# Loading the second block's input first, and one square root for two norms, in a Mamba + MLP + mixture-of-experts kernel

## The chip, the cores and the metric

The kernel runs on one core of a Trainium2 chip. A core has a matrix engine (TensorE, PE in the profile, with its weight loads as PEld), a vector engine (VectorE, DVE), an engine for functions such as exp, silu and square root (ScalarE, ACT), a general engine (GpSimd, POOL) and a queue engine that here only issues transfers (SyncE, SP). Each takes its instructions in the order in which they stand in its queue; semaphores tie the engines together. The metric is the device time of one execution in microseconds (us).

## The reference

Input x is 2048 tokens by 512, all in float32. Cut to what matters:

```
x = x + ref1(layernorm(x))        # Mamba-2 block, then a gated MLP
x = x + ref2(layernorm(x))        # router, 8 experts, the best 2 of each token

ref1(h):
  r = h;  h = rmsnorm(h, ln1_w)
  z, xb, B, C, dt = split(h @ in_proj_w)
  xb, B, C = silu(causal_conv4([xb, B, C]))
  dt = softplus(dt + dt_bias);  A = -exp(A_log)
  y = scan over chunks of 128 tokens of (xb*dt, dt*A, B, C) + D*xb
  h = r + rmsnorm(y * silu(z), norm_w) @ out_proj_w
  return h + (silu(h2 @ gate_w) * (h2 @ up_w)) @ down_w,  h2 = rmsnorm(h, ln2_w)

layernorm(x)  = (x - mean) / sqrt(var + eps)
rmsnorm(h, w) = h / sqrt(mean(h*h) + eps) * w          # eps = 1e-5 in both
```

Two norms follow each other at the start: layernorm of x, then rmsnorm of its result. With v the variance of a token, layernorm scales by `rstd = 1/sqrt(v + eps)`. The mean square of its result is `v * rstd^2`, so both together scale by `rstd / sqrt(v * rstd^2 + eps)`. This is the same as `1 / sqrt(v * (1 + eps) + eps^2)`. The residual path needs `rstd` alone.

## The kernel before

The tokens are cut into 8 blocks of 256 (`TB`), each of two tiles of 128. The Mamba part runs block by block. For every group of 512 tokens (`FB`) the gated MLP and the router are interleaved, with one group's lag: while blocks 0 and 1 (the first group) run, there is no MLP work yet. After the last block come the rest of the MLP and the experts. The script names dependencies only; a planner puts the instructions of each engine in a fixed order ahead of the run, by its own model of times and by the order of the script. An instruction that the script has late can stand early in its queue when its inputs are ready early in that model.

The start, by lines:

- L79 to L100 issue the first loads on the queue of SP: two x tiles (`load_x`, L77, 256 KB each), the parameters (L86), the columns of w_in for dt (`w_dt`, L88), three column pairs of w_in (`load_w_in`, L93, 512 KB each, four buffers), two more x tiles for block 1, then `w_o` (L99, 2 MB) and the router's weights (L100).
- L135 and L136 compute `a_neg = -exp(A_log)`.
- `scales(b)` (L175) takes mean and variance of the block's two tiles into `mv` (`stats`, L148 and L149: DVE), then `rstd` (`rsqrt_eps`, L143: a square root on ACT, L144: a reciprocal on DVE), then `ms = v * rstd^2` (L181, L182), a second `rsqrt_eps` on it, and the product `rboth` (L184).
- `prepare(b)` (L196) is a generator: it calls `scales`, forms `hn = (x - mean) * rboth` (L203), transposes it on PE (L190) and multiplies by ln1_w into `hT` (L194). After a first yield come the projection for dt (`pdt`, L214) and softplus by a polynomial on DVE (L224 to L236), in which the Exp of L226 is the only work of ACT. After a second yield comes `dA = dt * a_neg` (L242), its sum along the chunk on PE (`pc`, L245), and rows that go to memory and come back broadcast (`rowsd`, L250; `cum`, L279, masked on POOL in L281; `ec`, L291).
- `project` (L304) multiplies `hT` by one column pair of w_in (`pm`, L300), copies it to `pre` (L310, ACT), takes three halo columns from the pair's previous block and saves three for the next (L311, L312: POOL), convolves (L317, L319: DVE) and applies silu (L323: ACT). `gate` (L325) does the same product for z (`pz`).
- L457 scales `w_o` by norm_w on POOL, eight instructions, once.
- `chunk` (L338) runs the scan of one tile: `psc` (L361), the exponentials `cum` (L367: ACT, L369: DVE), `py` (L382, L388), `y` (L400, L404), squares on ACT (L424, L425), their sum over eight column groups on POOL (`sq`, L427) and over channels on PE (`pms`, L430), then the output projection `po` (L437). `h` of L439 is layernorm(x), with `rstd`; L440 adds the projection to it.

The loads of later blocks are issued in `mamba(b)`, two blocks ahead (L655). Block 0 is prepared before the loop over blocks (L642), and block b + 1 inside block b.

Of the kernel before, what the change touches and what calls it, by code (L numbers as in the profile page):

```python
# [8 lines left out]
F32 = mybir.dt.float32  # L9
I32 = mybir.dt.int32  # L10
AF = mybir.ActivationFunctionType
ALU = mybir.AluOpType
# [3 lines left out]
P = 128  # L16
# [5 lines left out]
NH = 16  # L22
HD = 64
TB = 256
NCH = TB // P
# [15 lines left out]
EPS = 1e-5  # L41


C_CW, C_CB, C_NW, C_D, C_L1, C_L2, C_DTB, C_AL = 0, 48, 60, 68, 76, 80, 84, 100
# [4 lines left out]
def mamba_mlp_moe(ctx, tc, x, w_in, w_out, w_gate, w_up, w_down, par, wr, wg, wu, wd, out):  # L49
# [3 lines left out]
    nc = tc.nc  # L53

    def bc(ap, axis, n):
        ap = ap.unsqueeze(axis)
        shape = list(ap.shape)
        shape[axis] = n
        return ap.to_broadcast(shape)


    const = ctx.enter_context(tc.tile_pool(name="const", bufs=1))
# [12 lines left out]
    def load_x(t):  # L75
        res[t] = xp.tile([P, D], F32, name=f"x{t}", tag="x")
        nc.sync.dma_start(out=res[t], in_=x[t * P : (t + 1) * P, :])  # L77

    params = const.tile([P, NPAR], F32, name="params")  # L79
# [1 line left out]
    w_o = pw.tile([P, 8, D], F32, name="w_o")  # L81
    wr_sb = const.tile([P, NK, NE], F32, name="wr_sb")

    for t in range(NCH):
        load_x(t)
    nc.sync.dma_start(out=params, in_=par)  # L86
    w_in_k = w_in.rearrange("(k p) n -> p k n", p=P)
# [2 lines left out]
    def load_w_in(pair):  # L90

        w = pw.tile([P, NK, 2 * P], F32, name="wi", tag="wi", bufs=4)
        nc.sync.dma_start(out=w, in_=w_in_k[:, :, pair * 2 * P : (pair + 1) * 2 * P])  # L93
        return w

    ahead = [load_w_in(pair) for pair in range(3)]
    for t in range(NCH, 2 * NCH):
        load_x(t)
    nc.sync.dma_start(out=w_o, in_=w_out.rearrange("(t p) n -> p t n", p=P))  # L99
    nc.sync.dma_start(out=wr_sb, in_=wr.rearrange("(k p) e -> p k e", p=P))  # L100

# [29 lines left out]
        out=upto, in_=ones[:, : NE * NE].rearrange("p (e f) -> p e f", e=NE), pattern=[[1, NE], [-1, NE]],  # L131
        compare_op=ALU.is_ge, fill=0.0, base=0, channel_multiplier=0,
    )
    a_neg = const.tile([P, NH], F32, name="a_neg")
    nc.scalar.activation(a_neg, params[:, C_AL : C_AL + NH], AF.Exp)  # L135
    nc.vector.tensor_scalar_mul(a_neg, a_neg, -1.0)  # L136
    mv = const.tile([P, NT, 2], F32, name="mv")
    rstd = const.tile([P, NT], F32, name="rstd")
    rboth = const.tile([P, NT], F32, name="rboth")

    def rsqrt_eps(dst, src, scale=1.0):

        nc.scalar.activation(dst, src, AF.Sqrt, bias=eps, scale=scale)  # L143
        nc.vector.reciprocal(dst, dst)  # L144

    def stats(pool, src, dst):
        st = pool.tile([P, 6], F32, name="bn", tag="bn")
        nc.vector.bn_stats(out=st, in_=src)  # L148
        nc.vector.bn_aggr(out=dst, in_=st)  # L149
# [7 lines left out]
    wa = pa_stack.enter_context(tc.tile_pool(name="wa", bufs=2))  # L157
# [14 lines left out]
        return pool.tile([P, *shape], F32, name=name, tag=tag)  # L172


    def scales(b):  # L175
        lo, hi = b * NCH, (b + 1) * NCH
        for t in range(lo, hi):
            stats(wa, res[t], mv[:, t, :])
        rsqrt_eps(rstd[:, lo:hi], mv[:, lo:hi, 1])
        ms = wa.tile([P, NCH], F32, name=f"ms{lo}", tag="ms")  # L180
        nc.vector.tensor_tensor(ms, mv[:, lo:hi, 1], rstd[:, lo:hi], ALU.mult)  # L181
        nc.vector.tensor_tensor(ms, ms, rstd[:, lo:hi], ALU.mult)  # L182
        rsqrt_eps(rboth[:, lo:hi], ms)
        nc.vector.tensor_tensor(rboth[:, lo:hi], rboth[:, lo:hi], rstd[:, lo:hi], ALU.mult)  # L184

    def transposed(src, dst, weight=None):

        pt = bank("tr", [NK, P], "pt")
        for k in range(NK):
            nc.tensor.transpose(pt[:, k, :], src[:, k * P : (k + 1) * P], ident)  # L190
        if weight is None:
            nc.scalar.copy(dst, pt)  # L192
        else:
            nc.vector.tensor_tensor(dst, pt, bc(weight, 2, P), ALU.mult)  # L194

    def prepare(b):  # L196

        scales(b)
        hT = wa.tile([P, NK, TB], F32, name=f"hT{b}", tag="hT")
        for j in range(NCH):  # L200
            t = b * NCH + j
            hn = wa.tile([P, D], F32, name=f"hn{t}", tag="tok", bufs=3)
            nc.vector.tensor_scalar(  # L203
                hn, res[t], mv[:, t, 0:1], rboth[:, t : t + 1], ALU.subtract, ALU.mult
            )
            transposed(hn, hT[:, :, j * P : (j + 1) * P], params[:, C_L1 : C_L1 + NK])

        yield hT


        pdt = ps_tr.tile([P, NCH, NH], F32, name=f"pdt{b}", tag="tr")
        for j in range(NCH):
            for k in range(NK):
                nc.tensor.matmul(  # L214
                    pdt[:, j, :], hT[:, k, j * P : (j + 1) * P], w_dt[:, k, :],
                    start=(k == 0), stop=(k == NK - 1),
                )

        def small(name, bufs=2):
            return wa.tile([P, NCH, NH], F32, name=f"{name}{b}", tag=name, bufs=bufs)  # L220

        v, u, s, s2, acc = (small(n, 1) for n in ("v", "u", "s", "s2", "acc"))
        dt = small("dt")
        nc.vector.tensor_tensor(v, pdt, bc(params[:, C_DTB : C_DTB + NH], 1, NCH), ALU.add)  # L224
        nc.vector.scalar_tensor_tensor(u, v, -1.0, v, ALU.mult, ALU.min)
        nc.scalar.activation(u, u, AF.Exp)  # L226
        nc.vector.tensor_scalar_add(s, u, 2.0)
        nc.vector.reciprocal(s, s)
        nc.vector.tensor_tensor(s, s, u, ALU.mult)
        nc.vector.tensor_tensor(s2, s, s, ALU.mult)  # L230
        nc.vector.tensor_scalar_mul(acc, s2, 1.0 / 17.0)
        for c in (15.0, 13.0, 11.0, 9.0, 7.0, 5.0, 3.0):
            nc.vector.scalar_tensor_tensor(acc, acc, 1.0 / c, s2, ALU.add, ALU.mult)
        nc.vector.scalar_tensor_tensor(acc, acc, 1.0, s, ALU.add, ALU.mult)
        nc.vector.tensor_scalar_max(dt, v, 0.0)
        nc.vector.scalar_tensor_tensor(dt, acc, 2.0, dt, ALU.mult, ALU.add)  # L236

        yield


        dA = small("dA")
        nc.vector.tensor_tensor(dA, dt, bc(a_neg, 1, NCH), ALU.mult)  # L242
        n = NCH * NH
        pc = ps_tr.tile([P, P], F32, name=f"pc{b}", tag="tr")
        nc.tensor.matmul(pc[:n], dA.rearrange("p j h -> p (j h)"), tri, start=True, stop=True)  # L245
        rows = wa.tile([n, 2, P], F32, name=f"rows{b}", tag="rows", bufs=1)
        nc.vector.tensor_copy(rows[:, 0, :], pc[:n])
        nc.scalar.activation(rows[:, 1, :], pc[:n], AF.Exp)
        rows_d = scratch.tile([2, n, P], F32, name=f"rowsd{b}", tag="rowsd", bufs=NB)
        nc.sync.dma_start(out=rows_d.rearrange("a n q -> n a q"), in_=rows)  # L250

        pn = ps_tr.tile([P, NCH, NH], F32, name=f"pn{b}", tag="tr")
        nc.tensor.transpose(pn.rearrange("p j h -> p (j h)"), rows[:, 0, :], ident[:n, :n])
        ncum = small("ncum")
        nc.vector.tensor_scalar_mul(ncum, pn, -1.0)

        yield

        dtdec = small("dtdec")
        psum = ps_tr.tile([P, 2, NCH, NH], F32, name=f"psum{b}", tag="tr")  # L260
        nc.tensor.matmul(psum[:, 0], late, dA, start=True, stop=True)
        nc.tensor.matmul(psum[:, 1], ones, dA, start=True, stop=True)
        nc.scalar.activation(dtdec, psum[:, 0], AF.Exp)
        nc.vector.tensor_tensor(dtdec, dtdec, dt, ALU.mult)
        cd = wa.tile([P, NCH, 2, 4], F32, name=f"cd{b}", tag="cd")
        for half in range(2):
            part = slice(half * HD, (half + 1) * HD)
            tot = psum[part, 1].rearrange("p j (g h i) -> p j g h i", g=2, h=2)
            nc.scalar.activation(cd[part], tot[:, :, :, half, :], AF.Exp)
        return hT, dt, ncum, dtdec, cd, rows_d  # L270
# [364 lines left out]
    def finish(steps):  # L635
        while True:
            try:
                next(steps)
            except StopIteration as end:
                return end.value  # L640

    ready = finish(prepare(0))  # L642
    near = [spread(0, j, ready[-1]) for j in range(NCH)]

# [297 lines left out]
```

## Time and profile before

| | us |
|---|---|
| median of 3 runs | 1644.21 (1644.12 to 1644.91) |
| profiled execution, its own time | 1643.64 |
| its span, first to last instruction | 1641.9 |
| PE busy | 1589.6 |
| DVE busy | 706.2 |
| ACT busy | 597.1 |
| POOL busy | 299.4 |
| first matmul or transpose on PE | 13.29 |

The span is what the profile shows; the execution's time is 1.7 us longer. Busy time is summed over the whole span, and the stages differ: at the start and in blocks 0 to 3 several engines are close to full, later PE alone is. Rows of the timeline give start and duration in us, the engine, the line, the operation, what it writes and reads, and how many instructions are merged; in brackets stands how long the engine was idle before it, and what ended that wait. SPq and the like are an engine's queue issuing a transfer. PEclk is the clock of PE that was granted, as a share of full speed.

### The profile page before, as it was taken

The numbers are of one execution on the slowest core, as the hardware profiler recorded it, in microseconds if no ns is written. First come the engines' busy times: TensorE is split into PE (matmuls) and PEld (weight loads), VectorE is DVE, ScalarE is ACT, GpSimd is POOL, SyncE is SP. The second block draws the span as 40 slices with busy tenths as digits, with TensorE's granted clock in tenths as the row PEclk, the third lists the DMA queues.
The fourth block names the chain that finished last, engine by engine and source line by source line (L and its number), as shares of the span: only waits on it lengthen the run. The fifth ranks groups of instructions, "written<-read, shape, count | busy, mean of one in ns | idle before, by whom it ended". The sixth has DMA issues, their size and how long they took to land.

```text
span 1641.9 us, 16534 instructions
## 1 busy us (share of the span) xinstructions
PE 1589.6 (97%) x5515; PEld 909.0 (55%) x5515; DVE 706.2 (43%) x1835; ACT 597.1 (36%) x1033; POOL 299.4 (18%) x349
## 2 busy tenths in 40 slices
PE   6989899999999999999999999999999999999997
PEld 5656565555556655655565555445444655555553
DVE  6776654534445365535544642323421441111111
ACT  4978774435243533353344334112000211111110
POOL 4332211211021102111201110000010123232221
PEclk9999899999999999999999999999999999999999
DMA  7644333434234533333344321228763234333322
GB/s 250 190 115 130 112 116 113 122 91 122 78 115 129 174 97 90 103 110 109 90 146 150 110 71 58 64 64 265 225 206 116 71 58 73 63 59 63 64 40 32
DMA packets 165203, 182.87 MB, mean 111 GB/s; under 512 B 10432, under 2 KB 125632, under 8 KB 165120
## 3 DMA queue, kind: packets, MB, share of 16 engines
q1 hardware_dynamic: 147456, 145.10, 29.9%
q0 software_dynamic: 8736, 20.45, 7.3%
q10 hardware_dynamic: 8928, 16.26, 2.7%
q8 instruction: 46, 0.75, 0.2%
q14 instruction: 37, 0.30, 0.1%
HBM read 155.04 MB, written 26.74 MB: 111 GB/s over the span
## 4 chain that ended last, share of the span: by engine, by line
PE 85%; DMA 4%; issue 4%; ACT 2%; DVE 2%; POOL 1%; SPq 0%; POOLq 0%; DVEq 0%; ACTq 0%
PE pg L592 13%; PE pd L603 13%; PE pu L592 13%; PE pm L300 9%; PE po L437 6%; PE pz L300 5%; PE epd L832 5%; PE epg L817 4%; PE epu L817 4%; DMA out<-ey,idx 3%; PE py L388 2%; PE psc L361 2%; PE py L382 2%; PE pt L190 2%; PE pls L579 1%
## 5 line engine op out<-in xcount | busy, mean ns | idle before, releaser
L592 PE MATMUL pg<-h2T,mg 128*128 128x512 f32 x512 | 231.8, 593 | 0.0
L592 PE MATMUL pu<-h2T,mu 128*128 128x512 f32 x512 | 230.2, 592 | 0.0
L603 PE MATMUL pd<-md,a 128*128 128x512 f32 x512 | 225.4, 592 | 0.0
L300 PE MATMUL pm<-hT,wi 128*128 128x256 f32 x768 | 183.4, 391 | 0.0
L595 DVE TENSOR_TENSOR a<-a,pu 128x512 f32<-128x512 f32 x64 | 44.0, 688 | 285.3 <-PE pu L592 275.8
L603 PEld LDWEIGHTS pd<-md,a 128*128 128x128 f32 x512 | 97.1, 190 | 122.3 <-issue 120.1
L592 PEld LDWEIGHTS pu<-h2T,mu 128*128 128x128 f32 x512 | 97.2, 190 | 122.0 <-issue 117.9
L300 PEld LDWEIGHTS pm<-hT,wi 128*128 128x128 f32 x768 | 145.8, 195 | 34.0 <-issue 12.6
L592 PEld LDWEIGHTS pg<-h2T,mg 128*128 128x128 f32 x512 | 96.1, 190 | 98.6 <-issue 96.3
L606 DVE TENSOR_TENSOR r<-r,pd 128x512 f32<-128x512 f32 x128 | 87.9, 687 | 116.1 <-PE pd L603 115.2
L319 DVE SCALAR_TENSOR_TENSOR ca<-pre,params,ca 128x256 f32<-128x256 f32 x288 | 129.3, 507 | 0.6
L832 PE MATMUL epd<-ew,ehT 128*128 (+1 forms) x234 | 110.2, 607 | 8.5 <-DVE ehT L828 8.5
L437 PE MATMUL po<-w_o,y 128*128 128x512 f32 x256 | 118.4, 610 | 0.0
L817 PE MATMUL epg<-ew,xgT 128*128 x312 | 118.1, 460 | 0.3 <-ACT xgT L192 0.3
L817 PE MATMUL epu<-ew,xgT 128*128 x312 | 117.7, 459 | 0.0
L300 PE MATMUL pz<-hT,wi 128*128 128x256 f32 x512 | 115.1, 381 | 0.0
L300 PEld LDWEIGHTS pz<-hT,wi 128*128 128x128 f32 x512 | 95.5, 190 | 13.6 <-issue 0.8
L819 ACT ACTIVATE eh<-epg 128x352 f32<-128x352 f32 x39 | 18.1, 465 | 218.7 <-PE epg L817 218.7
L367 ACT ACTIVATE cum<-cum,ncum 128x128 f32<-128x128 f32 x256 | 85.1, 391 | 24.1 <-POOL cum L281 23.5
L594 ACT ACTIVATE a<-pg 128x512 f32<-128x512 f32 x64 | 37.7, 588 | 151.8 <-PE pg L592 134.9
L838 POOL DMA_INDIRECT out<-ey,idx x39 | 61.8, 1584 | 160.3 <-DVE ey L837 146.4
L367 ACT ACT_TABLE_LOAD x65 | 83.4, 1283 | 1.6 <-issue 0.6
(220 smaller groups left out, 1777.1 us busy)
## 6 DMA issues: line engine op xcount, KB each, us to landing
wi<-in_w_in SPq DMA_DIRECT2D x80, 512.0 KB, 3.8
mg<-in_w_gate SPq DMA_DIRECT2D x64, 256.0 KB, 2.9
mu<-in_w_up SPq DMA_DIRECT2D x64, 256.0 KB, 2.9
md<-in_w_down SPq DMA_DIRECT2D x64, 256.0 KB, 2.8
cum<-rowsd SPq DMA_DIRECT2D x32, 512.0 KB, 4.8
ec<-rowsd SPq DMA_DIRECT2D x60, 128.0 KB, 4.1
xnd<-xn ACTq DMA_DIRECT2D x28, 256.0 KB, 3.9
ew<-in_wg SPq DMA_DIRECT2D x8, 704.0 KB, 5.5
```

The source lines that it names most:

```text
L300: nc.tensor.matmul(pm[:, m, :], w[:, k, m * P : (m + 1) * P], hT[:, k, :], start=(k == 0), stop=(k == NK - 1))
L319: nc.vector.scalar_tensor_tensor(ca, pre[:, m, k : k + TB], cw[:, k : k + 1], ca, ALU.mult, ALU.add)
L367: nc.scalar.activation(lt[:, half, i], lt[:, half, i], AF.Exp, bias=ncum[:, j, h : h + 1])
L437: nc.tensor.matmul(po, y[:, m, :], w_o[:, m, :], start=(m == 0), stop=(m == 7))
L592: nc.tensor.matmul(ps, wt[:, k, :], hT[:, k, :], start=(k == 0), stop=(k == NK - 1))
L594: nc.scalar.activation(a, pg, AF.Silu)
L595: nc.vector.tensor_tensor(a, a, pu, ALU.mult)
L603: nc.tensor.matmul(pd, a[:, j * P : (j + 1) * P], d, start=(m == 0), stop=(m == len(held) - 1))
L606: nc.vector.tensor_tensor(rows[j], rows[j], pd, ALU.add)
L817: nc.tensor.matmul(ps, xT[:, k, :], w[:, lo : lo + EI], start=(k == 0), stop=(k == NK - 1))
L832: nc.tensor.matmul(pd, hT[:n, m, :], w[:n, NG + m * D : NG + (m + 1) * D], start=(m == 0), stop=(m == len(ET) - 1))
L838: nc.gpsimd.indirect_dma_start(out=out, out_offset=bass.IndirectOffsetOnAxis(ap=idx[:, n : n + 1], axis=0), in_=y, in_offset=None, compute ...
```

## The change

The x tiles of block 1 are loaded together with those of block 0, ahead of the parameters and of w_in. `scales` computes `rboth` directly, with one square root of `v * (1 + eps) + eps^2` and one reciprocal; the constant eps^2 is a new small tile set on POOL. `rstd` is computed by its own square root and reciprocal after the first yield of `prepare`, for every block. `a_neg` is computed in the preparation of block 0, after the second yield, in place of the beginning.

```
-    for t in range(NCH):
+    for t in range(2 * NCH):
         load_x(t)
     nc.sync.dma_start(out=params, in_=par)
...
     ahead = [load_w_in(pair) for pair in range(3)]
-    for t in range(NCH, 2 * NCH):
-        load_x(t)
     nc.sync.dma_start(out=w_o, in_=w_out.rearrange("(t p) n -> p t n", p=P))
...
+    eps2 = const.tile([P, 1], F32, name="eps2")
+    nc.gpsimd.memset(eps2, EPS * EPS)
     a_neg = const.tile([P, NH], F32, name="a_neg")
-    nc.scalar.activation(a_neg, params[:, C_AL : C_AL + NH], AF.Exp)
-    nc.vector.tensor_scalar_mul(a_neg, a_neg, -1.0)
...
     def scales(b):
         lo, hi = b * NCH, (b + 1) * NCH
         for t in range(lo, hi):
             stats(wa, res[t], mv[:, t, :])
-        rsqrt_eps(rstd[:, lo:hi], mv[:, lo:hi, 1])
-        ms = wa.tile([P, NCH], F32, name=f"ms{lo}", tag="ms")
-        nc.vector.tensor_tensor(ms, mv[:, lo:hi, 1], rstd[:, lo:hi], ALU.mult)
-        nc.vector.tensor_tensor(ms, ms, rstd[:, lo:hi], ALU.mult)
-        rsqrt_eps(rboth[:, lo:hi], ms)
-        nc.vector.tensor_tensor(rboth[:, lo:hi], rboth[:, lo:hi], rstd[:, lo:hi], ALU.mult)
+        nc.scalar.activation(rboth[:, lo:hi], mv[:, lo:hi, 1], AF.Sqrt, bias=eps2, scale=1.0 + EPS)
+        nc.vector.reciprocal(rboth[:, lo:hi], rboth[:, lo:hi])
...
         yield hT
+        lo, hi = b * NCH, (b + 1) * NCH
+        rsqrt_eps(rstd[:, lo:hi], mv[:, lo:hi, 1])
...
         yield
+        if b == 0:
+            nc.scalar.activation(a_neg, params[:, C_AL : C_AL + NH], AF.Exp)
+            nc.vector.tensor_scalar_mul(a_neg, a_neg, -1.0)
```

## The prediction

> **What bounds the kernel now.** I read the page first, then busy time by stretch, then the chain of work that ended last, then the start engine by engine, and the waits of TensorE last. The page, engine rows and TensorE by slice:
>
> ```profile
> PE 1589.6 (97%) x5515; PEld 909.0 (55%) x5515; DVE 706.2 (43%) x1835; ACT 597.1 (36%) x1033; POOL 299.4 (18%) x349
> ...
> PE   6989899999999999999999999999999999999997
> ```
>
> TensorE (PE) works 1589.6 of 1641.9 us, so at most 52.3 us can be won. Where its idle time lies, by stretches (busy us of PE, PEld, DVE, ACT, POOL; then clock and DMA):
>
> ```profile
> 0.00:13.29 13.29, 0.00 (x1) 0.04 (x1) 4.73 (x21) 3.37 (x5) 4.68 (x20) 1.00 0.84 270
> 13.29:60.80 47.51, 45.81 (x215) 37.78 (x215) 38.55 (x102) 32.41 (x48) 23.47 (x26) 1.00 0.79 237
> ...
> 112.10:121.00 8.90, 4.30 (x10) 2.86 (x10) 3.37 (x5) 4.42 (x7) 5.32 (x7) 0.67 0.00 0
> ...
> 203.00:1280.00 1077.00, 1075.49 (x3556) 586.07 (x3554) 477.21 (x1235) 384.29 (x645) 135.44 (x176) 1.00 0.40 120
> ```
>
> From 203 to 1280 us PE misses 1.5 us: whatever VectorE (DVE) or ScalarE (ACT) save there is worth nothing. The idle time that the change can reach is the first 13.29 us and the waits before 203. The chain that ended last starts so:
>
> ```profile
> 4.36 6.75 DMA x<-in_x
> 11.13 0.69 DVE bn L148
> ...
> 15.28 3.59 PE pdt L214 x16
> 18.87 5.67 PE pm L300 x16
> ```
>
> The first thing that PE waits for is thus the second block's input, loaded behind three w_in tiles, although block 0 does not need it. DVE, which takes its queue in order, shows why:
>
> ```profile
> 11.13 0.69 DVE L148 BATCH_NORM_STATS2 bn<-x 128x6 f32<-128x512 f32 x1 [3.61 <-DMA x<-in_x]
> 11.74 0.15 DVE L144 RECIPROCAL rboth<-rboth 128x2 f32<-128x2 f32 x1
> ...
> 12.61 0.53 DVE L203 TENSOR_SCALAR hn<-x,mv,rboth 128x512 f32<-128x512 f32 x1
> ```
>
> Block 0's scale (L144) has its root from ACT at 7.85, but stands behind block 1's statistics, which wait for the load.
>
> **The x loads moved.** The queue of SP now issues x0, x1, parameters, w_dt, three w_in, x2, x3; later it is x0 to x3 and then the rest. An issue takes 0.42 to 0.56 us. From 5 to 20 us the DMA runs at 345 to 377 GB/s; take 360, so a 256 KB tile is 0.73 us. x0 was used at 3.56 and x1 at 4.38, so x2 should land near 5.1 and x3 near 5.8, in place of 11.11. Everything they overtake comes up to 1.45 us later: parameters 4.84 to 6.3 (next needed by hT, near 9), w_dt 5.6 to 7.0 (needed near 10). The third w_in: 2.7 MB in front of or in it, 7.5 us at 360, from 2.3 us on: near 10, needed after 13. All are covered; without that cover it is 1.45 us once. w_o, 2 MB, has the same bytes in front of it as before, so its landing, 18.85, does not move.
>
> **One root, and Exp later.** Block 0's chain loses one root (0.29), one reciprocal and three small multiplies (0.13 to 0.17 each). Dropping the A_log Exp from the front also takes a table switch out of the path:
>
> ```profile
> 4.84 0.21 ACT L135 ACTIVATE a_neg<-params 128x16 f32<-128x16 f32 x1 [2.77 <-DMA params<-in_par]
> 5.35 1.28 ACT L143 ACT_TABLE_LOAD   x1 [0.29 <-DVE mv L149]
> 6.64 0.29 ACT L143 ACTIVATE rstd<-mv,eps 128x2 f32<-128x2 f32 x1
> ```
>
> Without Exp the root's table can load at 0.79, and the root follows mv (done at 5.26): ready at 5.6. DVE then does block 1's statistics first if they stay ahead in its queue: x2 until 6.0, x3 until 6.7, an aggregate, reciprocal at 6.9, hn at 7.1. If they do not, hn starts at 5.85. Against 12.61 that is 5.5 or 6.8 us; I take **5.5**, since one of them is ahead now. From hn to pdt the trace needs 15.28 - 12.61 = 2.7 us, so pdt starts near 9.8 and pm near 13.4.
>
> Moving Exp (0.21) and its -1 multiply (0.18) behind dt costs nothing: they are needed by dA (29.29, later 23.8), and ACT is idle for most of the stretch 20 to 28. If Exp needs a table of its own there, 1.28 us, that idle time holds it. The memset of eps2 on POOL is like that of eps, 0.09 us, in front of an idle queue.
>
> rstd still takes a root and a reciprocal, now behind the yield, for h (L440, 82.44 for the first): slack everywhere. Per block there are as many roots, but they no longer depend on each other and can share a table. For block 2 they are now apart, at 37.71 and 42.01, each with a load before and one after; if adjacent, ACT saves 2 x 1.28 = 2.6 us. The Trainium skill (ScalarE: Activation LUTs, What ACT_TABLE_LOAD costs) prices a switch at 1.283 us plus a drain, 2.66 together, which would make it 5.3. The row decides: after the load that starts at 40.72, the root starts at 42.01, with no drain between. I use 1.28.
>
> **What takes the gain back.** The 5.5 us pass on through pdt, dt and dA up to the second column pair of w_in. Its convolution on DVE (L317) waits for the halo copy on POOL, and that stands behind the scaling of w_o:
>
> ```profile
> 18.85 13.42 POOL L457 TENSOR_SCALAR w_o<-w_o,params 128x512 f32<-128x512 f32 x8 [13.52 <-DMA w_o<-in_w_out]
> 32.23 0.19 POOL L312 COPY halo<-pre 128x6 f32<-128x6 f32 x1
> 32.35 0.19 POOL L311 COPY pre<-halo 128x6 f32<-128x6 f32 x1
> ```
>
> ```profile
> 32.58 0.36 DVE L317 TENSOR_SCALAR ca<-pre,params 128x256 f32<-128x256 f32 x1 [0.16 <-POOL pre L311]
> ```
>
> Today this wait is 0.16 us, because statistics of block 2 fill the time. It starts with w_o's landing, which doesn't move; so DVE would arrive near 27 and wait until 32.5. Behind L317 on DVE queue all later convolutions, for which ACT's silu and then PE's psc and py wait. After 32.58 DVE is nearly full until 57.7. What it can still win there is its idle time of 0.82 and 0.69 us (both waiting for ACT, which now is ahead) and four instructions of 0.16: **2.2 us**. If instead the pair's halo copies get in front of w_o, the third pair stops instead: w_o from 20.1 to 33.5, its halo copy at 33.8 against a convolution at 36.73 now: 2.9, plus 0.69 and 0.64, **4.2 us**. The order on POOL can't be read from this trace, so I take the middle, rounded down: **3.0 us**. PE gives back the other 2.5 in waits before psc (49.55) and py (62.29).
>
> Here a rule speaks against the change. The skill (TensorE: Matmul & The Clock Gate, Part 1: The HAM clock gate) says that an idle window of about 3.4 us halves PE's clock until it has been busy as long. The trace agrees at 112 us:
>
> ```profile
> 116.75 0.58 PE L430 MATMUL pms<-ones,sq 128*128 128x1 f32 x2 [4.60 <-POOL sq L427]
> 117.19 2.05 PE L437 MATMUL po<-w_o,y 128*128 128x512 f32 x2
> 119.04 5.08 PE L300 MATMUL pm<-hT,wi 128*128 128x256 f32 x16
> ```
>
> Sixteen pm take 4.89 us in the chain here and 3.54 elsewhere, and two po 1.9 in place of 0.9: 2.4 us of penalty; the wait of 1.5 us before 62.29 brings none. The new waiting is about 2.5 in two pieces, with 1.5 there already, so by the row it costs nothing. By the rule, in one piece it would cost 2.4, leaving 0.6. This is the low end.
>
> **Sum.** Against the profiled execution, 1641.9 of span and 1.7 around it, 1643.64 in all: minus 3.0 is 1640.6. The median of the runs is 0.57 above that execution, so **1641.2** against 1644.2. A difference of 0.2%, 3.3 us, is about what a measurement of this kernel can tell from no change. Its own range is 1639.8 to 1643.6.
>
> **Rivals.**
> *Full carry.* w_o's scaling does not hold the convolution (another order on POOL or DVE), and PE keeps 5.5: 1638.7. For it: PE itself is busy 45.8 of 47.5 us up to 60.8. Against: the 0.16 us wait, already there.
> *The later stalls shrink.* pms at 116.75 and at 197.5 waits for sq on POOL, behind cum (L281), which waits for its DMA. Should the new order put sq first for one, that is 4.6 + 2.4 = 7 more: 1634. The trace has such a case, sq at 152.39 ahead of cum at 161.48. Nothing in the edit aims at it.
> *Slower.* The same place in reverse: at 152 cum gets in front of sq. Then sq ends near 161.48 + 1.09 + 2.6 = 165.2 in place of 155.0; PE has other work for part of that, and I price it like the stall at 112, 7 us: 1641.2 + 7 = 1648. It decides once the new stall takes more than 3.0.
>
> **How the numbers follow.** Partly absorbed 0.55, full carry 0.17, stalls shrink 0.13, slower 0.15. Of the first, 0.4 lies over 3.3 us. Faster: 0.22 + 0.17 + 0.13 = 0.52; same: 0.33 and 0.03 of the slower case, 0.36; slower 0.12. The range, 1635.5 to 1645.5, leaves out about half of the shrunken stalls and two thirds of the slower case.
>
> **What would show it.** Right: the first hn near 7, first pm near 13.4; on DVE's first L317 of the second pair an idle of several us put down to POOL; PE's work at 62.29 only 2 to 4 us earlier; block 2's roots with one load between them; 203 to 1280 as full as now. Wrong: x3 landing after 7; the halo copies ahead of w_o on POOL; the stalls at 112 and 190 gone, longer, or joined by a third.

## The result, and the profile after

| | before | after |
|---|---|---|
| median of 6 runs, us | 1644.86 (1644.12 to 1645.2) | 1635.59 (1633.95 to 1639.16) |
| profiled execution, us | 1643.64 | 1635.68 |
| its span, us | 1641.9 | 1634.0 |
| PE busy, us | 1589.6 | 1587.6 |
| first transpose on PE, us | 13.29 | 10.14 |

The ratio is 0.9948, with a 95% interval of 0.9937 to 0.9960. The kernel is faster by 0.5%, some 8.6 us of the median before.

The page of the kernel after, its engine rows and TensorE by slice:

```profile
PE 1587.6 (97%) x5515; PEld 907.4 (56%) x5515; DVE 700.3 (43%) x1811; ACT 587.6 (36%) x1027; POOL 298.6 (18%) x350
...
PE   7989899999999999999999999999999999999997
```

The idle time of PE, span less busy, fell from 52.3 to 46.4 us; the other 2.0 us of the span are busy time that shrank, since PE worked less at half clock, as shown at the end of this section. Busy time by stretches after, in the columns of the prediction's view:

```profile
0.00:10.14 10.14, 0.00 (x1) 0.03 (x1) 4.71 (x18) 4.11 (x8) 4.71 (x21) 1.00 0.83 263
10.14:60.80 50.66, 48.91 (x225) 38.86 (x226) 37.58 (x106) 34.47 (x56) 22.55 (x26) 1.00 0.80 250
112.09:121.00 8.91, 8.91 (x34) 6.13 (x35) 3.00 (x8) 4.25 (x8) 1.82 (x3) 0.81 0.20 57
...
203.00:1280.00 1077.00, 1074.13 (x3532) 582.60 (x3531) 475.55 (x1221) 377.15 (x637) 134.84 (x174) 1.00 0.40 119
```

The empty stretch at the start is 3.15 us shorter. From 203 to 1280 us PE misses 2.9 us where it missed 1.5. Followed along PE's work, the change is ahead of the kernel before by: 3.2 us at the first transpose, 5.1 at the first `py` (62.29 to 57.17), 5.8 at the first `pms` (77.62 to 71.84), 4.7 at the second and at the third, 7.0 at the fourth (197.52 to 190.53), 8.9 at the first `pg`, the first product of the gated MLP (217.91 to 209.04), and 7.9 at the end. Not all of these marks have the same work in front: ahead of the first `py` the kernel before has done 48 `pz` and the change 44, ahead of the first `pms` 6 and 4 `po`, ahead of the third and the fourth two `po` fewer than the change. The `psc` behind the first `py` has the same work ahead of it in both, and comes at 63.49 and 59.24: 4.2 us earlier, and not 5.1.

Counted in PE's idle time, which does not hang on this order, 5.0 us are won up to the third `pms` at 150 (3.15 of them at the start), 2.05 between the third and the fourth, and 1.1 are lost after it. So there are two gains.

The start of ACT after:

```profile
0.79 1.28 ACT L237 ACT_TABLE_LOAD   x1 [0.79 <-PEq L931]
7.20 0.21 ACT L237 ACTIVATE a_neg<-params 128x16 f32<-128x16 f32 x1 [5.13 <-DMA params<-in_par]
7.43 1.28 ACT L141 ACT_TABLE_LOAD   x1
8.73 0.30 ACT L141 ACTIVATE rstd<-mv,eps 128x2 f32<-128x2 f32 x1
8.93 0.47 ACT L178 ACTIVATE rboth<-mv,eps 128x2 f32<-128x2 f32 x2
```

The Exp of A_log, which the script now has behind dt, still stands first in ACT's queue: its inputs, the parameters, are there early in the planner's model. The parameters land at 7.20, behind four x tiles (4.84 before, behind two), and the root waits for the Exp and a table load. The first `hn` follows at 9.45 instead of the predicted 7.1.

The place where the prediction expected the gain to be given back, DVE and POOL after:

```profile
32.57 0.62 DVE L317 TENSOR_SCALAR ca<-pre,params 128x256 f32<-128x256 f32 x2 [3.46 <-POOL pre L311]
```

```profile
19.10 13.17 POOL L457 TENSOR_SCALAR w_o<-w_o,params 128x512 f32<-128x512 f32 x8 [13.74 <-DMA wr_sb<-in_wr]
32.23 0.19 POOL L312 COPY halo<-pre 128x6 f32<-128x6 f32 x1
32.35 0.31 POOL L311 COPY pre<-halo 128x6 f32<-128x6 f32 x2
```

The wait of 0.16 us has become 3.46, at the predicted instruction and behind the predicted eight scalings. And yet PE comes out of this stage with more than it had at the start. ACT's rows say how. Block 2's roots before, each with a load of its own and another behind it (at 38.02 and 42.32) to go back to silu:

```profile
36.41 1.28 ACT L143 ACT_TABLE_LOAD   x1
37.71 0.29 ACT L143 ACTIVATE rstd<-mv,eps 128x2 f32<-128x2 f32 x1
...
40.72 1.28 ACT L143 ACT_TABLE_LOAD   x1
42.01 0.29 ACT L143 ACTIVATE rboth<-ms,eps 128x2 f32<-128x2 f32 x1
```

Block 2's roots after share one load, and one more goes back to silu:

```profile
32.44 0.59 ACT L310 COPY pre<-pm 128x512 f32<-128x512 f32 x1 [1.35 <-POOL halo L312]
33.05 1.28 ACT L178 ACT_TABLE_LOAD   x1
34.35 0.29 ACT L178 ACTIVATE rboth<-mv,eps 128x2 f32<-128x2 f32 x1
34.55 0.28 ACT L141 ACTIVATE rstd<-mv,eps 128x2 f32<-128x2 f32 x1
34.84 1.28 ACT L323 ACT_TABLE_LOAD   x1
36.14 0.91 ACT L323 ACTIVATE xb<-ca,params 128x256 f32<-128x256 f32 x2
```

The copy and both roots lie in the very time in which DVE waits for POOL. After this ACT is idle once until 57.5, for 1.24 us. The end of the first half's work on ACT before, DVE behind it, and PE behind DVE:

```profile
59.25 0.51 ACT L323 ACTIVATE cs<-ca,params 128x256 f32<-128x256 f32 x1
59.77 1.28 ACT L367 ACT_TABLE_LOAD   x1
61.07 0.98 ACT L367 ACTIVATE cum<-cum,ncum 128x128 f32<-128x128 f32 x3
```

```profile
61.50 0.93 DVE L369 SCALAR_TENSOR_TENSOR cum<-cum,dt,psc 128x128 f32<-128x128 f32 x3 [1.86 <-ACT cum L367]
62.29 1.27 PE L388 MATMUL py<-cum,xbt 128*64 128x512 f32 x4 [1.51 <-DVE cum L369]
```

and ACT after:

```profile
54.16 0.69 ACT L367 ACTIVATE cum<-cum,ncum 128x128 f32<-128x128 f32 x2
...
56.66 0.89 ACT L323 ACTIVATE cs<-ca,params 128x256 f32<-128x256 f32 x2
```

Before, PE's `py` waited for DVE, and DVE had waited 1.86 us for ACT: the last three exponentials stood behind the last silu and a table load. After, the eight exponentials of the first half are done at 54.85, ahead of the last two silus; both kinds are done at 57.55 in place of 62.05, and the wait before `py` is gone. Up to that point and after 20 us, ACT loads 13 tables in place of 14. Call this time, when ACT has done the twelve silus of block 0's convolution and the first half's eight exponentials, **ACT done**.

The fourth tile's stall, PE before and after:

```profile
197.52 0.59 PE L430 MATMUL pms<-ones,sq 128*128 128x1 f32 x2 [6.15 <-POOL sq L427]
```

```profile
190.53 0.38 PE L430 MATMUL pms<-ones,sq 128*128 128x1 f32 x2 [4.60 <-POOL sq L427]
```

POOL ahead of it, before and after:

```profile
189.49 1.26 POOL L281 TENSOR_SCALAR_AFFINE_SELECT cum<-cum 128x1024 f32<-128x1024 f32 x1 [7.01 <-DMA cum<-rowsd]
...
192.66 1.04 POOL L410 TENSOR_TENSOR state<-state,cd 128x512 f32<-128x512 f32 x1
...
194.88 2.59 POOL L427 TENSOR_TENSOR sq<-sq 128x512 f32<-128x512 f32 x3
```

```profile
176.14 1.15 POOL L410 TENSOR_TENSOR state<-state,cd 128x512 f32<-128x512 f32 x1
183.25 1.14 POOL L281 TENSOR_SCALAR_AFFINE_SELECT cum<-cum 128x1024 f32<-128x1024 f32 x1 [5.96 <-DMA cum<-rowsd]
...
187.88 2.59 POOL L427 TENSOR_TENSOR sq<-sq 128x512 f32<-128x512 f32 x3
```

From one `pms` to the next, third to fourth, it is 42.46 us before and 40.12 after. From the masking of `cum` to `sq` POOL takes 5.4 us before and 4.6 after: the state's product (L410), 1.04 us, now stands in POOL's idle time ahead of `cum`. The other 1.6 us is that `cum`'s rows land earlier, counted from the third `pms` (34.4 us before, 32.8 after).

Behind this stall PE works at half clock for a while. Granted clock (third figure from the end) in this stretch, before and after:

```profile
197.52:203.94 6.42, 6.42 (x12) 3.91 (x13) 1.37 (x3) 1.95 (x3) 1.34 (x1) 0.50 0.00 0
```

```profile
191.00:194.40 3.40, 3.40 (x7) 1.99 (x7) 1.37 (x3) 1.89 (x3) 0.89 (x1) 0.50 0.00 0
```

At the stall of the second tile it is 5.28 us at half clock before (116.75 to 122.03) and 3.41 after. Half of such time is lost: some 5.8 us before and 3.4 after. The lower clock thus accounts for about 2.4 us of the difference between these two executions, beside the 5.9 us of idle time; the sum, 8.3, is 0.4 above the 7.9 of the span. Not all of the 2.4 is the edit's: a second execution of the same order of instructions (the Exp at its old place, below) has PE at half clock for 5.1 and 4.4 us at these two stalls, a loss of 4.75.

### The profile page after: what moved, and what is told of

Its sections match the earlier page's. It is cut to its first block, busy times and chain, and to the rows that moved or that the text cites. A ratio compares the mean times of both kernels' runs of the same rounds, so it can differ in the third digit from the quotient of the medians.

```text
span 1634.0 us, 16508 instructions
## 1 busy us (share of the span) xinstructions
PE 1587.6 (97%) x5515; PEld 907.4 (56%) x5515; DVE 700.3 (43%) x1811; ACT 587.6 (36%) x1027; POOL 298.6 (18%) x350
## 4 chain that ended last, share of the span: by engine, by line
PE 84%; DMA 6%; issue 4%; POOL 2%; ACT 2%; DVE 1%; SPq 0%; POOLq 0%; DVEq 0%; ACTq 0%
PE pu L592 13%; PE pg L592 13%; PE pd L603 13%; PE pm L300 8%; PE po L437 6%; PE pz L300 6%; PE epd L832 5%; PE epu L817 4%; PE epg L817 4%; DMA out<-ey,idx 3%; PE psc L361 2%; PE py L388 2%; PE py L382 2%; PE pt L185 2%; PE pls L579 1%
```

## The experiments

Ratios are against runs of the kernel before on the same chip, taken together with them, so they, not the medians, are compared. Line numbers shift by a few in these kernels. Landmarks in us, from the one profiled execution of each:

| kernel | first pt | ACT done | first py | 1st pms | 4th pms | median | ratio (95%) |
|---|---|---|---|---|---|---|---|
| before | 13.29 | 62.05 | 62.29 | 77.62 | 197.52 | | 1 |
| after | 10.14 | 57.55 | 57.17 | 71.84 | 190.53 | 1635.59 | 0.9948 (0.9937 to 0.9960) |
| x loads only | 10.81 | 61.58 | 61.81 | 77.14 | 196.3 | 1643.03 | 0.9995 (0.9988 to 1.0001) |
| no x move | 8.01 | 60.32 | 59.82 | 74.49 | 194.52 | 1637.09 | 0.9958 (0.9945 to 0.9972) |
| Exp at its old place | 9.65 | 58.14 | 57.73 | 72.4 | 191.49 | 1636.6 | 0.9960 (0.9947 to 0.9974) |
| parameters third | 9.28 | 57.60 | 57.11 | 71.78 | 192.6 | 1637.61 | 0.9966 (0.9952 to 0.9980) |
| w_o scaled later | 9.46 | 57.05 | 56.55 | 71.23 | 189.46 | 1634.47 | 0.9944 (0.9931 to 0.9958) |
| two sums on DVE | 9.12 | 57.80 | 57.30 | 71.97 | 186.93 | 1630.75 | 0.9923 (0.9910 to 0.9937) |
| second root dependent | 9.92 | 61.44 | 62.88 | 77.01 | 197.23 | 1642.18 | 0.9987 (0.9980 to 0.9993) |
| no roots | 10.12 | 60.36 | 63.31 | 79.54 | 197.02 | 1643.78 | 0.9994 (0.9986 to 1.0002) |
| w_o later, two sums on DVE | 9.65 | 56.71 | 56.29 | 70.97 | 185.46 | 1629.49 | 0.9912 (0.9896 to 0.9927) |
| before, sixth pair late | 13.35 | 64.96 | 58.40 | 80.4 | 199.07 | 1642.34 | 0.9993 (0.9984 to 1.0001) |
| x loads only, sixth pair late | 10.44 | 64.14 | 57.92 | 77.1 | 196.41 | 1641.11 | 0.9986 (0.9980 to 0.9993) |
| the two edits, two pairs late | 9.79 | 62.02 | 54.46 | 75.43 | 187.92 | 1630.58 | 0.9920 (0.9906 to 0.9933) |

The columns for `py` and the first `pms` compare only kernels with the same work in front. Ahead of the first `py` there are 48 `pz` in the kernel before, with the x loads only, with the dependent root and with no roots; 44 in the change and in those that keep its order; 32 in the last three rows. Ahead of the first `pms` there are 6, 4, and 8 `po` (12 in the last row).

The theories: that the start's gain passes on, less what the halo wait takes (the prediction); that the gain comes from the root, through ACT's table loads; and that it comes from the order of exponentials and silus on ACT, which the root only happens to change.

**The x loads alone**, on the kernel before:

```
-    for t in range(NCH):
+    for t in range(2 * NCH):
         load_x(t)
...
-    for t in range(NCH, 2 * NCH):
-        load_x(t)
```

> Before plus the moved x loads alone; both roots and the Exp stay as they were. Theory (the earlier start comes from the loads, what is won after it comes from the single root): the roots still stand behind the Exp, which now waits longer for the parameters, so hn starts near 10.6 in place of 12.6; start gain 2 us, no relief on ACT later, so 2 to 3 us faster than before, near 1642.5. Rival (the loads do all of it): 8 to 9 us faster, near 1636. Rival (the single root does all of it): no change, 1645.

Ratio 0.9995: no change that can be measured. PE starts 2.5 us earlier, and 0.5 is left at the first `py`. ACT of this kernel shows where the rest goes:

```profile
34.77 0.51 ACT L321 ACTIVATE xb<-ca,params 128x256 f32<-128x256 f32 x1 [1.60 <-DVE ca L317]
...
45.35 0.51 ACT L321 ACTIVATE cs<-ca,params 128x256 f32<-128x256 f32 x1 [1.73 <-DVE ca L317]
```

ACT's first silu is 2.1 us earlier than before (27.84 for 29.92), and these two waits for the convolution give it all back. They stand in front of a stretch in which ACT is full until 61.58. PE's own wait stands there too, for ACT's copy `xbt`, at a place where the kernel before has none:

```profile
46.88 0.66 PE L188 MATMUL pt<-ident,hn 128*128 128x128 f32 x4 [2.96 <-ACT xbt L348]
```

So of the earlier start by itself nothing is measured at the end, and by the interval it is worth 2 us at most.

**The change without the x move:**

```
-    for t in range(2 * NCH):
+    for t in range(NCH):
         load_x(t)
...
     ahead = [load_w_in(pair) for pair in range(3)]
+    for t in range(NCH, 2 * NCH):
+        load_x(t)
```

> The changed kernel with block 1's x loads put back behind w_in; single root and Exp as in the change. Theory: hn of block 0 is early (near 7.5) but hT stands behind block 1's statistics on DVE, which wait for the load until 11.1, so pdt starts near 13.3 against 15.3 before and 12.0 after; with the relief on ACT later 5 to 6 us faster than before, near 1639.5, and 3 to 4 slower than the change. Rival (the loads do all of it): near 1645. Rival (the single root does all of it): 1636.

Ratio 0.9958: most of the gain is there without any x tile moved. The landmarks of this kernel are from an execution of 1640.66 us, 3.6 over its own median, so they are not leaned on. Its interval overlaps that of the whole change; whether the x move adds up to 2 us on top of the root is not settled.

**The change with the Exp at its old place in the script:**

```
+    nc.scalar.activation(a_neg, params[:, C_AL : C_AL + NH], AF.Exp)
+    nc.vector.tensor_scalar_mul(a_neg, a_neg, -1.0)
...
-        if b == 0:
-            nc.scalar.activation(a_neg, params[:, C_AL : C_AL + NH], AF.Exp)
-            nc.vector.tensor_scalar_mul(a_neg, a_neg, -1.0)
```

> The change without its third edit: the exponential of A_log stays where it was in the code. Theory (the planner puts it at the front either way): the same as the whole change, ratio 0.9948 within 0.001, first pt at 9.5 to 10.5. Rival (the third edit does something): first pt or the end differs by more than 1 us.

The planner gives this script the same order of instructions on every engine as the changed kernel. The ratio, 0.9960, has an interval around 0.9948; the two are one program measured twice, and differ by 1.0 us of median and 0.5 us in the first `pt`. The third edit does nothing, and differences of a microsecond or two between the kernels of this table say nothing.

**The parameters as the third load,** the change otherwise:

```
     for t in range(2 * NCH):
         load_x(t)
-    nc.sync.dma_start(out=params, in_=par)
+        if t == NCH - 1:
+            nc.sync.dma_start(out=params, in_=par)
```

> The changed kernel with the parameters' load issued third, behind x0 and x1 and ahead of x2 and x3; the order of the other engines stays. Theory (the Exp, still ahead of the roots on ACT, holds them until the parameters land): the Exp runs near 5.3 in place of 7.2, the first hn near 7.9 in place of 9.45, and the 1.5 us pass on: near 1634. Rival (what is won at the start is taken back at the halo copies behind w_o's scaling, which end at 32.4 in any case): no change against the change, 1635.6, with the wait of 3.46 us before the convolution grown to 5.

PE starts 0.4 to 0.9 us earlier than in the two executions of the change's own order, and at the first `py` nothing of it is left (57.11). The rival's wait is where it was expected, and as large:

```profile
33.08 0.62 DVE L318 TENSOR_SCALAR ca<-pre,params 128x256 f32<-128x256 f32 x2 [5.00 <-POOL pre L312]
```

The late parameters are a real loss at the start; once it is removed, the wait for the halo copies takes the gain back. The ratio's interval, 0.9952 to 0.9980, overlaps that of the change.

**The scaling of w_o issued behind the first half of chunk 1,** the change otherwise:

```
-    for m in range(8):
-        nc.gpsimd.tensor_scalar_mul(w_o[:, m, :], w_o[:, m, :], params[:, C_NW + m : C_NW + m + 1])
...
+                if b == 0 and n == 1:
+                    for m in range(8):
+                        nc.gpsimd.tensor_scalar_mul(w_o[:, m, :], w_o[:, m, :], params[:, C_NW + m : C_NW + m + 1])
```

> The changed kernel with the scaling of w_o written later in the script, so that on POOL one of its eight instructions comes before the second pair's halo copy in place of all eight; six still come before the third pair's. No other engine's order changes. Theory A (POOL's scaling of w_o is what holds the stretch up to the first py): the convolution of the second pair starts near 27.5 in place of 32.6, its wait of 3.46 us is gone, py comes 3 us earlier and the end with it: near 1632.5. Theory B (ACT's table loads hold it): py within 0.7 us of where it is, no change of the end.

The convolution's wait for POOL is gone, and in its place, on DVE, stands:

```profile
30.72 1.08 DVE L317 TENSOR_SCALAR ca<-pre,params 128x256 f32<-128x256 f32 x2 [2.13 <-ACT pre L310]
```

It starts 1.9 us earlier, not 5, because it now waits for ACT's copy; the first `py` gains 0.6 and the ratio, 0.9944, can't be told from that of the change. Taking the halo wait away does not move the end by an amount that can be measured here: ACT is the next in line.

**The sums of tiles 1 and 3 on DVE,** the change otherwise:

```
-            nc.gpsimd.tensor_tensor(sq[:, 0:n, :], sq[:, 0:n, :], sq[:, n : 2 * n, :], ALU.add)
+            eng = nc.vector if t in (1, 3) else nc.gpsimd
+            eng.tensor_tensor(sq[:, 0:n, :], sq[:, 0:n, :], sq[:, n : 2 * n, :], ALU.add)
```

> The changed kernel with the three sums of squares of tiles 1 and 3 on DVE in place of POOL. Theory (the two waits of 4.5 us of PE, at 112 and 190, are POOL's queue alone, and the slow clock after them is their echo): both waits go, with 1.3 to 2 us of slow matmuls after each: 10 to 12 us faster than the change, near 1625. Rival (PE is held by the squares themselves or by something that is late next, such as cum): less than 4 us faster.

Ratio 0.9923, some 4 us better than the change. PE's waits at these two tiles:

```profile
110.86 0.38 PE L431 MATMUL pms<-ones,sq 128*128 128x1 f32 x2 [2.43 <-DVE sq L428]
...
186.93 0.38 PE L431 MATMUL pms<-ones,sq 128*128 128x1 f32 x2 [2.48 <-DVE sq L428]
```

4.45 and 4.60 us became 2.4 and 2.5. The 10 to 12 us that were expected did not come: the waits are halved, not gone, and PE still works 3.4 us at half clock after each, as in the change. Some 2 us of each stall are thus POOL's queue; what is left waits for DVE. No other stage moved (first `py` 57.30).

**Two roots that depend on each other,** the change otherwise; the first `rboth` still needs one root only, but `rstd`'s root takes its input through a product with zero times `rboth`:

```
-        rsqrt_eps(rstd[:, lo:hi], mv[:, lo:hi, 1])
+        nc.vector.scalar_tensor_tensor(rstd[:, lo:hi], rboth[:, lo:hi], 0.0, mv[:, lo:hi, 1], ALU.mult, ALU.add)
+        rsqrt_eps(rstd[:, lo:hi], rstd[:, lo:hi])
```

> The changed kernel with the root for rstd made to depend on rboth by a small DVE instruction (it adds zero times rboth to the variance), so that the two roots of a block can no longer stand next to each other; rboth is still one root. Theory B (what the single root gave is one pair of table loads less on ACT ahead of the first py): block 2's roots are apart again, py 3 to 4 us later, near 61, and the end 3 to 5 us later than the change, near 1639.5. Rival (it is the shorter chain to hn): no change against it, 1635.6.

This keeps the start (first `pt` 9.92) and loses nearly the whole gain: 0.9987. The roots of block 2 stand 4.3 us apart again (38.01 and 42.31), each with a load before and one after, and ACT is done at 61.44. Two rows show what is lost, ACT's wait for a convolution and PE's for ACT:

```profile
35.58 0.51 ACT L324 ACTIVATE xb<-ca,params 128x256 f32<-128x256 f32 x1 [5.08 <-DVE ca L320]
```

```profile
46.74 1.11 PE L185 MATMUL pt<-ident,hn 128*128 128x128 f32 x4 [4.97 <-ACT xbt L351]
```

In the changed kernel ACT fills the halo wait with a copy, a load and both roots. Here it stands idle through that wait, and then spends four loads on the two roots, where the change spends two. PE's wait is followed by half clock (0.50 from 46.74 to 49.50), which costs this execution another 1.4 us. So the root at the start is not what pays; what pays is that the two roots of a block are independent of each other.

**No root on ACT at all:** both scales by three Newton steps on DVE, from the start value 1. This stands only for variances near 1, as this input has them.

```
-        nc.scalar.activation(rboth[:, lo:hi], mv[:, lo:hi, 1], AF.Sqrt, bias=eps2, scale=1.0 + EPS)
-        nc.vector.reciprocal(rboth[:, lo:hi], rboth[:, lo:hi])
+        nwt(rboth[:, lo:hi], mv[:, lo:hi, 1], f"nb{lo}", 1.0 + EPS, EPS * EPS)
...
-        rsqrt_eps(rstd[:, lo:hi], mv[:, lo:hi, 1])
+        nwt(rstd[:, lo:hi], mv[:, lo:hi, 1], f"ns{lo}", 1.0, EPS)
```

> The changed kernel with rboth and rstd by three Newton steps on DVE from a start of 1, good only for variances near one as this input has; ACT takes no root for the first norms. Theory B: eleven table loads fewer on ACT, the pair ahead of the first py among them; py 2 to 3 us earlier than in the change, near 54.5, end near 1633. Theory A: py stays near 57, since DVE still waits for the halo copies until 32.5; end unchanged.

Ratio 0.9994: fewest table loads of all (180 in the whole program, against 191 in the change and 197 with the x loads alone), and no gain. The saving is not in the stretch that counts: from 20 us to ACT done there are 14 loads, as before, against 13 in the change. And DVE adds a delay:

```profile
62.74 0.16 DVE L180 TENSOR_TENSOR ns<-rstd 128x2 f32<-128x2 f32 x1
62.82 0.60 DVE L378 SCALAR_TENSOR_TENSOR cum<-cum,dt,psc 128x128 f32<-128x128 f32 x2
```

The last two `cum` of the first half, whose exponentials were done at 60.36, stand on DVE behind Newton steps for a later block. PE waits 3.89 us for them before `py` (63.31), and works at half clock until 68.30, another 2.5 us lost in this execution. The theory that counts loads falls as a rule for the whole kernel: what counts is what stands in front of `py`, on either engine. Loads in that stretch alone are not tested by this kernel.

**Both good edits together,** w_o's scaling later and the two sums on DVE:

```
-    for m in range(8):
-        nc.gpsimd.tensor_scalar_mul(w_o[:, m, :], w_o[:, m, :], params[:, C_NW + m : C_NW + m + 1])
...
+            eng = nc.vector if t in (1, 3) else nc.gpsimd
...
+                if b == 0 and n == 1:
+                    for m in range(8):
+                        nc.gpsimd.tensor_scalar_mul(w_o[:, m, :], w_o[:, m, :], params[:, C_NW + m : C_NW + m + 1])
```

> The changed kernel with w_o's scaling later and the sums of squares of tiles 1 and 3 on DVE. If the two gains are independent: what the later scaling gives (0 by theory B, 3 by theory A) plus the 4 us that the sums on DVE gave: 1631.5 by B, 1628.5 by A.

Ratio 0.9912, 1629.49 us: the lowest median of the case, 14.5 us under the kernel before by the ratio. Against the sums alone the intervals overlap, and so theories A and B are not told apart by it.

**The sixth column pair late, on the kernel before.** This moves one pair's projection, convolution and silus behind the first half of chunk 0, so that ACT has the exponentials ahead of the last silus without any part of the change:

```
-    for pair in range(6):
+    for pair in range(5):
...
+                if b == 0 and n == 0:
+                    for pair in range(5, 6):
+                        project(0, pair, hT, xb, cs)
```

> The kernel before, no part of the change in it: only the projection and convolution of the first block's sixth column pair is issued after the first half of chunk 0 instead of ahead of it, so that the planner puts the first half's eight exponentials in front of the last two silus of the convolution on the scalar engine. Theory (the order of exponentials and silus decides when the first y product starts): first y product at 58 to 60 us instead of 62.3, ratio 0.997 to 0.998 (1639 to 1641 us). Rival (only the single square root moves the end): first y product at 62, ratio 1.000 within 0.0015.

The first `py` is where the theory put it, 58.40, and the end is not: 0.9993. PE of this kernel:

```profile
58.40 2.17 PE L388 MATMUL py<-cum,xbt 128*64 128x512 f32 x4 [1.11 <-DVE cum L369]
60.49 7.89 PE L300 MATMUL pz<-hT,wi 128*128 128x256 f32 x26
```

PE reached `py` earlier by leaving out sixteen `pz` (32 in front of it, where the kernel before has 48), which it does behind it; and ACT's queue became longer, not shorter: it is done at 64.96, with 15 table loads after 20 us instead of 14. The first `pms` is 2.8 us later than before, but this execution can't say what the order costs: it is the slowest but one of 13 (1644.20, their median is 1642.34), and PE is at half clock from 57.8 to 64.6, which takes 3.1 us; four `py` take 2.17 us here and 1.08 in the change. By the median of 13 the order gives no gain that can be measured, where 3 to 5 us were expected. The theory that the order of exponentials and silus alone decides has fallen in that size, and with it the first `py` as a mark: it is comparable only between kernels with the same work in front of it.

**The same with the x loads first:**

```
-    for t in range(NCH):
+    for t in range(2 * NCH):
         load_x(t)
```

> The same with the second block's input loads ahead of the weights, and still two separate roots. Theory: with the good order the earlier start passes to the end, so another 2.5 us off: first y product at 56 to 57.5, ratio 0.9955 to 0.9965 (some 1637 us), against 0.9995 for the same loads in the old order. Rival (the earlier start passes only with the single root): the same as the kernel with the late column pair alone.

Ratio 0.9986, with an interval that overlaps those of the kernel with the late pair alone and of the x loads alone. Here too the start's 2.9 us reach `py` as 0.5. The median is 1.2 us below that of the late pair alone, so with two dependent roots at most a part of the start's gain passes, in either order.

**The two good edits, and two pairs late:**

```
-    for pair in range(6):
+    for pair in range(4):
...
+                if b == 0 and n == 0:
+                    for pair in range(4, 6):
+                        project(0, pair, hT, xb, cs)
```

> The change with the scaling of w_o issued later, the sums of squares of tiles 1 and 3 on the vector engine, and the fifth and sixth column pairs projected after the first half of chunk 0. Theory: the first y product needs only the first four pairs' silus and the first half's exponentials, so it starts at 52 to 55 instead of 56.3 and the end is at 0.989 to 0.991 (1626 to 1629.5). Rival (the tensor engine is then given the same work later and waits there): no better than 0.9912, the same two edits without the late pairs.

The first `py` starts at 54.46, 1.8 us earlier than with the two edits alone, and the end is no better (0.9920). The first `pms` is 4.5 us later, with eight more `po` in front of it, 3.6 us of work. The rival was right.

**What follows.** Shown: the single root, with the second one independent, is worth nearly all of the gain; the x loads alone nothing that can be measured, the Exp nothing. Among the kernels that keep the work in its order and leave DVE alone, ACT done goes with the end: 62.05, 61.58 and 61.44 with ratios of 1, 0.9995 and 0.9987; 57.05 to 58.14 with 0.9944 to 0.9966. The change without the x move lies between (60.32, in an execution of 1640.66). That ACT's queue is the path from 33 to 58 us is thus read from traces: PE's waits of 2.96 and 4.97 us for ACT's copy `xbt`, where the change has 0.73 (at 43.69), point the same way; but the other execution of the change's order has 2.52 there. No run lengthens that queue by a known amount. How the gain divides between the table loads saved, the halo wait that the roots fill, and the order of exponentials and silus is open, and so is why `cum`'s rows land 1.6 us earlier at the fourth tile.

## Why the prediction was right, and where not

The forecast, 1641.2, was 5.6 us too slow. Faster was the likeliest side, and the measured 1635.59 lies in the range by 0.1 us, far outside the likeliest case's own range of 1639.8 to 1643.6: its mechanism was incomplete. That the number still falls in the range is luck. The range reached down so far for a rival, stalls at `pms` that vanish, and this is not what happened.

- **The x loads moved.** x2 was used at 6.24 and x3 at 7.07, for the predicted 5.1 and 5.8; the parameters were used at 7.20 for 6.3. All later by about 1, so that x3 is at the edge of what the prediction named as a sign of being wrong. The estimate used 360 GB/s; the trace of after moves 317 GB/s between 2.3 and 7.2 us.
- **One root, and Exp later.** The root was expected at 5.6 and came at 8.73, because the Exp did not move. A start gain of 3.2 in place of 5.5; the first `pm` started at 15.45, for the predicted 13.4. The prediction took the script's order for the queue's order in the one place where its own description says that the planner is free.
- **Block 2's roots share a table.** Right, and priced right: the activation follows 1.30 us after its load begins, 33.05 to 34.35, with no drain. But the 2.6 us saved were never put into the sum. This is the step that failed: ACT was counted as "now ahead", and the row that says otherwise, DVE waiting 1.86 us for ACT at 61.50, is in the trace of before. The prediction stopped at PE's wait of 1.51 for DVE and did not ask what DVE waited for.
- **What takes the gain back.** Right in place (L317, all eight scalings first), wrong in effect. DVE came to it at 29.1, not near 27, as the start had gained less; so the wait was 3.46 us, not 5.5. The price was set on DVE's queue; the queue that sets the pace behind it is ACT's, and ACT filled this wait with a copy and two roots, and had a shorter way after it. With the same work done, at the `psc` behind `py`, PE is 4.2 us earlier: more than at the start, where the prediction had less, and just outside its 2 to 4. Its own range for this case, 1639.8 to 1643.6, goes 0.2 us below what its larger price of 4.2 us gives, 1640.0.
- **The clock.** No new penalty at `py` in the change, as said. At 112 us the granted clock is low after 4.45 us of waiting, as before, but for less of PE's work (0.81 in the stretch, 0.67 before). The prediction held the old penalties fixed; the two stalls cost 2.4 us less in this execution, and 1.1 less in the other one of the same order. An idle window of 3.4 us was not needed: with the two sums on DVE, waits of 2.43 and 2.48 us were followed by half clock too, and with the sixth pair late one of 1.11 us, behind the narrow products `pdt`.
- **The later stalls.** The one at 112 carries on, as said. The stretch that ends with the one at 197 lost 2.3 us, the wait itself 1.55 (6.15 to 4.60). The rival "the later stalls shrink" had 7 us for one of them, by `sq` in front of `cum`; what happened is smaller and other: the state's product moved out of the way, and `cum`'s rows came earlier.
- **203 to 1280.** As full as before within 1.4 us, and that on the losing side.

The sum by what was measured: 4.7 us carried to the third `pms`, 2.3 at the fourth, 1.9 more by the first `pg`, 1.0 lost after it: 7.9 of the span. The prediction had 3.0, 0, 0 and 0. The 1.9 hold 1.5 us of half clock that is not paid (3.40 for 6.42 us) and two `po` that stand on the other side of the mark.

## What to carry to other kernels

Follow a wait back until an engine that waited for nothing: PE waited for DVE, but DVE for ACT, and only there does a saving count. When two activations of one table in a latency-bound stretch depend on each other through another engine, make them independent: here this let one table load serve both, in a wait that was there anyway, and was worth more than a start 2.5 us earlier. Before reading a gain off two traces, count what stands in front of the mark in each, and look where the granted clock is halved. Where a planner orders the queues, look at its order of the changed script before pricing an edit that only moves a line.

## What the runs showed of the hardware that was not expected

The same program, measured twice, started its first transpose at 10.14 and at 9.65 us, and its medians were 1635.59 and 1636.6. Six of the kernels have the change's order of instructions up to the first `hn`, and there the first transpose comes at 9.12 to 10.14, always 2.9 us after the parameters are used (6.18 to 7.20): it hangs on when that load lands. The runs of the changed kernel spread over 5.2 us; the 33 runs of the kernel before over 4.1 in one later measurement and over 6.0 in another. A single execution can't show an edit of 2 us.

Up to 1600 us, each stretch of half clock in these traces lasts 3.41, 6.83 or 10.24 us: once, twice or three times the same step. The length of the wait alone does not say whether or for how long. In the change 4.45 us of waiting bring 3.41 us of half clock, in the other execution of the same order 4.21 us bring 6.8, of which PE works in 5.1; 2.43 us bring 3.4 with the two sums on DVE, and 2.96 us none with the x loads alone (clock 1.00 from 46.88 to 52).
